# A graph network on one core: fewer column copies on ScalarE, and the placing of a chunk's sums ahead of the first layer

## The chip, the core and the metric

The kernel runs on one core of a Trainium2 chip. A core has TensorE (PE in the profile; its weight loads are PEld), VectorE (DVE), ScalarE (ACT), GpSimd (POOL) and SyncE (SP), which issues DMAs. Each engine takes its instructions in the order of its own program and waits on semaphores for the others. The metric is the device time of one execution in microseconds (us), lower is better.

## What is computed

One message-passing layer over a graph of 12,500 nodes with 128 features and 412,500 edges, sorted by their target node. The reference, cut to what matters (`x` has 32 scalars and 32 vectors of three a node):

```python
f0 = x0 @ W1_0e / np.sqrt(MUL)                      # and f1 from x1 with W1_1o
e0, e1 = feat0[edge_src], feat1[edge_src]           # rows gathered per edge
h = gelu(edge_scalar_attr @ W_mlp1 / np.sqrt(RADIAL))
h = gelu(h @ W_mlp2 / np.sqrt(HID))
w00, w01, w10, w11 = h @ Wp_00, h @ Wp_01, h @ Wp_10, h @ Wp_11
out0_a = w00 * e0 * ea0
out0_b = w11 * jnp.sum(e1 * ea1[:, None, :], -1) * INV_SQRT3
out1_a = (w01 * e0)[:, :, None] * ea1[:, None, :]
out1_b = w10[:, :, None] * e1 * ea0[:, :, None]
...
n0 = segment_sum(mid0, edge_dst) / np.sqrt(NUM_NEIGHBORS)   # and n1 from mid1
...
return layernorm(x + concat(y0, y1))
```

So each edge fetches the 128 features of its source node, multiplies them with weights that a small network makes of the edge's eight numbers, and adds the products to its target node.

## The kernel before

**Tiles.** The edges are cut into 806 runs of 512, a run into four quarters of 128 edges (one edge a partition). Two runs are a pair, four a chunk: 403 pairs and 202 chunks. The main loop `for p in range(NP)` handles one pair in each pass; `c` is the pair's chunk and `k` says whether the pair is the first (0, "even") or the second (1, "odd") of it. Four engines run an order that is written out by hand: what one pass calls, in the order in which it calls it, is each engine's program. POOL's gathers stand in the program's order too, ten pairs' buffers of G deep.

**Three ways to the source rows.** The features wanted by a quarter of a run normally come by one gather on POOL (`gather`, L223), which fetches 128 rows of a table in DRAM by their indices. A gather is issued nine pairs ahead, into the G buffer of the pair whose last message product has just been made, so the first gather of a pair waits for that product on VectorE. Every fourteenth run has one quarter fetched by SyncE with a DMA a row (`aid`, L208). And for some runs VectorE or ScalarE pick the columns themselves: all node features also lie transposed in SBUF (`xT`, a node a column), the address of a column is loaded into a register (`fetch`, L174), and a copy of one column of 128 numbers goes into a tile `gt` (`copy_columns`, L188 on VectorE, L192 on ScalarE). When a `gt` has its 128 columns, TensorE multiplies it with the weights and ScalarE copies the result into G (`picked_rows`, L197 and L198), and that quarter needs no gather.

**How many columns.** `SLOTS` says how many columns an engine copies in a pair, cut into slots between its other work, for even and odd pairs. `picked` is worked out from it at build time: from pair 6 on, an engine takes a further run as soon as its slots add up to 128 more columns. VectorE has 64 or 68 columns a pair and takes quarter 2 of a run now and then; ScalarE has 12, 16, 16 and 12 columns and takes quarter 1. `gather` leaves those quarters out.

**One pass for an even pair p = 2c,** with the lines as the profile names them:

- VectorE: `placing(c)` (L683) and `hot_rows(c + 1)` (L624); the first message product (L650); 24 columns; the second (L654); 20 columns; the third (L654); 20 columns. For an odd pair: the first two products; 24 columns; `select(c + 1)` (L639), which makes the segment weights of the next chunk; 16 columns; the third product; `add(c - 1)` (L710), which adds a placed chunk to the running sums; 28 columns.
- TensorE: `segments(p - 1)` (L670, 32 matmul records), `picked_rows` for runs two pairs ahead, `weights(p + 1)` (L597), `mlp1(c + 2)` (L554), then `place(c - 1)`, and now and then `moments` (L728, L731) of finished nodes. For an odd pair the second layer `mlp2(c + 2)` (L570) stands where `mlp1` stood, `radial` (L543) comes ahead of the weights, and there is no `place`.
- ScalarE: `segments_kept(p - 1)` (L676, copies the segment sums out of PSUM) with slot 0 of its columns; the copies into G (L198) and of the turned edge numbers (L545); slot 1; the first half of the layer's activation (`gelu1`, L559) with slot 2; `show(c + 1)` (L632, puts the edge attributes into PSUM for `select`); the second half of the activation with slot 3. For an odd pair the activation is `gelu2` (L576) and there is no `show`.

**`place(c)`** (L689 to L697) takes a chunk's four tiles of segment sums `SG` to their places among 96 nodes: it loads the four places into registers (L689), writes zeros with one matmul (L693), and adds four matmuls with the weights `SG` and the one-hot rows `PL` at places read from the registers (L697; eight matmul records). It writes into a PSUM tile called `bank` ("m" in the profile). The same tile holds the constant `numbers` (read by `placing` and `hot_rows`) and the area `shown` (written by `show`, read by `select`), and the order of use is kept for the tile as a whole: `select` waits for a `place` that stands ahead of it, and `place` for a `show` that stands ahead of it.

Of the kernel before, what the change touches and what calls it, by code (L numbers as in the profile page):

```python
# [15 lines left out]
ACT = mybir.EngineType.Activation  # L16
DVE = mybir.EngineType.DVE
# [28 lines left out]
AID_FROM = 36  # L46
AID_LEAD = 16
STEPS = 12
SLOTS = {DVE: ((24, 20, 20), (24, 16, 28)), ACT: ((12, 16, 16, 12), (12, 16, 16, 12))}
FROM = {DVE: 6, ACT: 6}  # L50
COL_Q = {DVE: Q - 2, ACT: Q - 3}
A_OF = (1, 2, 3, 0)
# [5 lines left out]
def gnn_kernel(ctx: ExitStack, tc: tile.TileContext, x, src, dst, ea4, ea8, w1_0, w1_1, wm1, wm2,  # L58
# [53 lines left out]

    per_chunk = {e: sum(map(sum, slots)) for e, slots in SLOTS.items()}
    picked = {}
    for e, slots in SLOTS.items():
        picked[e], done = [], 0
# [268 lines left out]
    for b in range(NG):  # L385
        c = math.ceil((min((b + 1) * GN, N) + MARGIN) / N * NCH) - 1
# [34 lines left out]
    def new_sums():  # L421
        A["next"] = wk.tile([P, 4, ACC], F32, name="acc")
# [519 lines left out]
    with tc.manual_schedule(engines={PE, ACT, DVE, SP}):  # L942
        load_raw_rows(nc.sync, 0, min(3, raw_runs))
        load_w1(nc.scalar)
        if raw_runs > 3:
            load_raw_rows(nc.scalar, 3, raw_runs)
        for s in range(min(LEAD - 2, raw_runs)):
            gather(s)
        nc.vector.tensor_scalar(ident, diag, 0.0, None, op0=OP.is_equal)
        nc.vector.tensor_copy(none[:, :P], iota)  # L950
        nc.vector.tensor_copy(bank[:, 4 * SPAN:4 * SPAN + P // 2], none[:, :P].bitcast(F32))
        for b in range(min(3, NG)):
            XT[b] = load_nodes(b)
        make_wf()
        clear()
        loads = list(weight_loads())
        new_sums()
        extra = {2: lambda: load_edges(0), 3: lambda: load_attributes(0), NG // 2 - 2: lambda: turn_attributes(0), 4: lambda: load_raws(0), NG // 2: lambda: load_indices(0),
                 NG // 2 + 3: make_w1b, NG // 2 + 5: make_ws, NG - 6: lambda: radial(0), NG - 4: lambda: networks(0),
                 NG - 2: lambda: networks2(0), NG - 1: make_wpost,  # L960
                 NG // 2 + 1: lambda: nc.vector.memset(A["next"], 0.0),
                 NG - 3: run_places}
        for b in range(NG + 2):
            if b < NG:
                turn(b)
            if 0 < b <= NG:
                features_of(b - 1)
            if 1 < b:
                store_nodes(nc.scalar, table, b - 2, PF[b - 2])
            if b + 3 < NG:  # L970
                XT[b + 3] = load_nodes(b + 3)
            if b > 4 and loads:
                nc.sync.dma_start(*loads.pop(0))
            if b in extra:
                extra[b]()
        assert not loads
        for c in range(1, min(EDGES_AHEAD, NCH)):
            load_edges(c)
        if aided:
            aid_load()  # L980
        for s in range(min(LEAD - 2, raw_runs), min(LEAD, NS)):
            gather(s)
        for c in range(1, min(3, NCH)):
            radial(c)
            if c == 1:
                networks(c)
                networks2(c)
        weights(0)
        show(0)
        hot_rows(0)  # L990
        select(0)
        for s in range(PR):
            turn_rows(s)
        for s in range(PR):
            features(s)
        A["now"] = A["next"]
        clearing = []
        placed = added = 0

        def picks(e, p, i, op=None):  # L1000
            if p < FROM[e]:
                if op:
                    op()
                return
            n = SLOTS[e][p % (CH // PR)][i]
            if not op:
                copy_columns(e, fetch(e, n))
                return
            first = fetch(e, n // 8 * 4)
            op()  # L1010
            copy_columns(e, first + fetch(e, n - n // 8 * 4))

        for p in range(NP):
            c, k = divmod(p, CH // PR)
            mine = [s for s in range(p * PR, (p + 1) * PR) if s < NS]
            if p:
                for s in mine:
                    if s + LEAD - PR < NS:
                        gather(s + LEAD - PR)
            if k == 1 and c + EDGES_AHEAD < NCH:  # L1020
                load_edges(c + EDGES_AHEAD)
            for s in mine:
                if s % P == P // 2 - 16 and (s // P + 1) * P < NS:
                    load_raws(s // P + 1)
                if s % P == P // 2 and (s // P + 1) * P < NS:
                    load_indices(s // P + 1)
                if s % ET == 8 and s - 8 + ET < NS:
                    load_attributes(s // ET + 1)
                for t in range(P // ROWS):
                    a = s + AID_LEAD - t * STEPS // (P // ROWS)  # L1030
                    if a in aided:
                        aid(a, t)
            nets = c + 2 < NCH
            if k == 0:
                placing(c)
                if c + 1 < NCH:
                    hot_rows(c + 1)
            if p:
                segments(p - 1)
                picks(ACT, p, 0, lambda: segments_kept(p - 1))  # L1040
            for e in picked:
                for s in mine:
                    if (e, s + 2 * PR) in pick_of:
                        picked_rows(e, pick_of[e, s + 2 * PR])
            if k == 1 and c + 3 < NCH:
                radial(c + 3)
            cleared = bool(late)
            rest = list(kept)
            norm_kept()
            picks(ACT, p, 1)  # L1050
            if p + 1 < NP:
                weights(p + 1)
            if nets:
                (mlp1, mlp2)[k](c + 2)
                picks(ACT, p, 2, lambda: (gelu1, gelu2)[k](c + 2, 0))
            else:
                picks(ACT, p, 2)
            if k == 0 and c + 1 < NCH:
                show(c + 1)
            for s in mine:  # L1060
                if s % ET == 20 and s - 20 + ET < NS:
                    turn_attributes(s // ET + 1)
            if nets:
                picks(ACT, p, 3, lambda: (gelu1, gelu2)[k](c + 2, 1))
            else:
                picks(ACT, p, 3)
            if k == 0 and c > 0:
                place(c - 1)
                placed = c
            raws_next = [s + PR for s in mine if s + PR < raw_runs]  # L1070
            for s in raws_next:
                turn_rows(s)
            messages(p, 0)
            if k == 0:
                picks(DVE, p, 0)
            messages(p, 1)
            picks(DVE, p, 1 - k)
            for s in raws_next:
                features(s)
            if rest:  # L1080
                norm_rest()
            if cleared:
                new_sums()
                clearing += list(range(4))
            elif clearing:
                clear_sums(clearing.pop(0))
            if k == 1 and c + 1 < NCH:
                select(c + 1)
            if k == 1:
                picks(DVE, p, 1)  # L1090
            messages(p, 2)
            if k == 1 and placed > added:
                add(added)
                added += 1
            picks(DVE, p, 2)
            if k == 0 and 0 < added == c - 1:
                norm(due.get(added - 1, []))
            if p == 0:
                addresses()
                find_first()  # L1100
                new_sums()
                clearing = list(range(4))
            if p == NP - 4:
                count_odd()
        finish_waiting()
        segments(NP - 1)
        segments_kept(NP - 1)
        if late:
            norm_kept()
            new_sums()  # L1110
            clearing += list(range(4))
        norm_rest()
        finish_waiting()
        for i in clearing:
            clear_sums(i)
        for c in range(added, NCH):
            if c >= placed:
                place(c)
            add(c)
            if c < NCH - 1 and c in due:  # L1120
                norm(due[c])
                norm_kept()
                norm_rest()
                finish_waiting()
        norm_last(due[NCH - 1])
# [31 lines left out]
```

## Time and profile before

| | us |
|---|---|
| runs of the kernel before | 5955.32, 5994.51, 5994.96 |
| median of them | 5994.51 |
| the profiled execution | 5962.68 |
| its span, first to last instruction | 5960.8 |
| mean granted clock of TensorE in it | 0.65 |

The profile's page gives busy time per engine, the chain of waits that ended last, and groups of instructions: line, engine, operation, tile written and tiles read, count, then total busy time and the mean of one in ns, then the idle time of the engine just ahead of them with what ended it. "Issue" there means that nothing in the profile explains the idle time; "remote" that a semaphore was raised by something that could not be told. A row of the timeline has the start and length in us, the engine and line, the count of merged instructions and, in brackets, the idle time before them and what ended it. POOL's gathers have rows of their own; the SyncE rows are left out of what is shown here, as are the weight loads of the timeline.

The profile's SyncE view holds 7040 single-row DMAs of `aid` (L208) beside the 2722 gathers by POOL from the table and 72 from the input.

### The profile page before, as it was taken

The numbers are of one execution on the slowest core, as the hardware profiler recorded it, in microseconds if no ns is written. First come the engines' busy times: TensorE is split into PE (matmuls) and PEld (weight loads), VectorE is DVE, ScalarE is ACT, GpSimd is POOL, SyncE is SP. The second block draws the span as 40 slices with busy tenths as digits, with TensorE's granted clock in tenths as the row PEclk, the third lists the DMA queues.
The fourth block names the chain that finished last, engine by engine and source line by source line (L and its number), as shares of the span: only waits on it lengthen the run. The fifth ranks groups of instructions, "written<-read, shape, count | busy, mean of one in ns | idle before, by whom it ended". The sixth has DMA issues, their size and how long they took to land. (4 is left out here: it accounts for less than half of the span.)

```text
span 5960.8 us, 141936 instructions
## 1 busy us (share of the span) xinstructions
PE 3407.7 (57%) x30231; PEld 2603.1 (44%) x30231; DVE 3366.2 (56%) x28706; ACT 3093.4 (52%) x24111; POOL 2636.3 (44%) x2801
## 2 busy tenths in 40 slices
PE   3665655556555555555556555556655555655556
PEld 2544444444444444444444444444434444443444
DVE  1265656555655555656555665566565555665556
ACT  0254555555555555555555555555554555555554
POOL 4344444444444444444444444444444444444441
PEclk5766666666666666666666666666666666666666
DMA  4211111111111111111111111111111111111111
GB/s 100 59 36 40 39 35 38 41 35 43 42 35 39 39 37 43 40 35 36 36 41 37 40 43 38 37 40 40 41 40 35 35 38 38 40 40 34 40 33 23
DMA packets 576979, 239.04 MB, mean 40 GB/s; under 512 B 481402, under 2 KB 526570, under 8 KB 576106
## 3 DMA queue, kind: packets, MB, share of 16 engines
q0 software_dynamic: 89408, 183.29, 10.8%
q1 hardware_dynamic: 465928, 40.14, 5.4%
q10 hardware_dynamic: 20770, 6.47, 0.5%
q14 instruction: 629, 5.15, 0.3%
q8 instruction: 244, 4.00, 0.3%
HBM read 216.86 MB, written 12.99 MB: 39 GB/s over the span
## 5 line engine op out<-in xcount | busy, mean ns | idle before, releaser
L223 POOL DMA_INDIRECT G<-table,idx x2722 | 2567.2, 943 | 3208.9 <-issue 1313.3
L192 ACT ACTIVATE gt<-xT 128x1 f32 x21888 | 2329.1, 189 | 924.5 <-issue 889.3
L188 DVE COPY gt<-xT 128x1 f32 x25984 | 1891.8, 145 | 1565.0 <-issue 1520.5
L670 PE MATMUL seg<-M,S 128*32 128x128 f32 x12896 | 845.7, 371 | 444.2 <-issue 426.8
L597 PE MATMUL w<-wpb,h 64*128 64x128 f32 x6448 | 855.1, 388 | 383.7 <-issue 383.1
L597 PEld LDWEIGHTS w<-wpb,h 64*128 64x128 f32 x6448 | 699.0, 277 | 554.6 <-issue 544.1
L670 PEld LDWEIGHTS seg<-M,S 128*32 128x32 f32 x12896 | 544.3, 148 | 692.1 <-issue 643.3
L654 DVE TENSOR_TENSOR M<-w,G 128x768 f32<-128x768 f32 x806 | 761.1, 945 | 2.7 <-issue 2.7
L676 ACT ACTIVATE sg<-seg 128x256 f32<-128x256 f32 x403 | 151.1, 375 | 1112.3 <-remote 777.6
L697 PEld LDWEIGHTS m<-pl,sg 128*128 128x128 f32 x1612 | 348.6, 312 | 797.7 <-issue 797.7
L693 PE MATMUL m<-none 128*128 128x384 bf16 x202 | 90.8, 450 | 786.1 <-ACT m L632 412.6
L554 PE MATMUL h<-eT,w1b 64*128 64x128 f32 x3232 | 439.3, 403 | 125.8 <-ACT G L198 95.9
L576 ACT ACTIVATE h<-h 128x512 f32<-128x512 f32 x404 | 237.1, 589 | 491.9 <-remote 377.0
L554 PEld LDWEIGHTS h<-eT,w1b 64*128 64x128 f32 x3232 | 394.3, 303 | 159.5 <-ACT G L198 120.5
L570 PE MATMUL h<-h,w2b 64*64 64x256 f32 x3232 | 393.5, 556 | 105.7 <-ACT G L198 68.7
L197 PE MATMUL h<-wf,gt 128*128 128x128 f32 x748 | 244.0, 411 | 268.2 <-issue 154.2
L650 DVE TENSOR_TENSOR M<-w,G 128x512 f32<-128x512 f32 x403 | 275.5, 684 | 204.1 <-remote 73.9
L697 PE MATMUL m<-pl,sg 128*128 128x128 f32 x1612 | 367.5, 404 | 0.0
L197 PEld LDWEIGHTS h<-wf,gt 128*128 128x128 f32 x748 | 162.8, 263 | 403.6 <-issue 246.9
L639 DVE TENSOR_TENSOR S<-oh,m 128x512 f32<-128x512 f32 x202 | 137.2, 679 | 356.7 <-PE m L697 251.4
L559 ACT ACTIVATE h<-h 128x512 f32<-128x512 f32 x404 | 234.6, 581 | 91.0 <-remote 37.9
L570 PEld LDWEIGHTS h<-h,w2b 64*64 64x64 f32 x3232 | 187.5, 186 | 214.9 <-ACT G L198 87.3
(123 smaller groups left out, 1592.5 us busy)
## 6 DMA issues: line engine op xcount, KB each, us to landing
G<-table SPq DMA_DIRECT2D x7040, 0.5 KB
G<-table,idx POOLq DMA_INDIRECT x2722
e<-in_edge_attr SPq DMA_DIRECT2D x201, 64.0 KB
xt<-in_x SPq DMA_DIRECT2D x24, 256.0 KB
table<-ft ACTq DMA_DIRECT2D x24, 256.0 KB
xt<-in_edge_attr SPq DMA_DIRECT2D x24, 256.0 KB
out<-y SPq DMA_DIRECT2D x24, 256.0 KB
xt<-in_dst SPq DMA_DIRECT2D x5, 256.0 KB
```

Of the source, the lines that this page charges most:

```text
L188: nc.vector.tensor_copy(to, col)
L192: nc.scalar.activation(to, col, AF.Copy)
L197: nc.tensor.matmul(pt, GT.pop((e, i)), wf, start=True, stop=True)
L223: nc.gpsimd.indirect_dma_start(out=G[s][:, q, :], out_offset=None, in_=x if s < raw_runs else table, in_offset=bass.IndirectOffsetOnAxis(a ...
L554: nc.tensor.matmul(p1[h][:, j // 2, j % 2, :], w1b[rows, j, :], eT[c][rows, :], start=True, stop=True)
L570: nc.tensor.matmul(p2[r][k * HID:(k + 1) * HID, h * n:(h + 1) * n], w2b[rows, :], H1[c][h][rows, k * n:(k + 1) * n], start=True, stop=True)
L576: nc.scalar.activation(H2[c][r].rearrange("p k j e -> p (k j e)"), P2[c][r], AF.Gelu_apprx_tanh, scale=1.0 / math.sqrt(HID))
L597: nc.tensor.matmul(WP[p][:, i, q, :], H2[c][q % 2][rows, k, q // 2, :], wpb[rows, :], start=True, stop=True)
L650: nc.vector.tensor_tensor(m[:, :, :, :MUL], w[:, :, :2 * MUL].rearrange("p q (a u) -> p q a u", a=2), g[:, :, None, :MUL].to_broadcast([P, ...
L654: nc.vector.tensor_tensor(m[:, :, j, MUL:].rearrange("p q (i u) -> p q i u", i=3), w[:, :, None, (2 + j) * MUL:(3 + j) * MUL].to_broadcast ...
L670: nc.tensor.matmul(SEG[c][q * W:(q + 1) * W, r + i, :], own[:, (r + i) * Q + q, h * W:(h + 1) * W], M[p][:, i, q, h, :], start=h == 0, sto ...
L697: nc.tensor.matmul(to[:, :, bass.ds(k_at, 4 * W)].bitcast(F32), SG[c][:, k, :], PL[c][:, k, :].rearrange("p (a n) -> p a n", a=4), start=F ...
```

## The change

Two edits. ScalarE's slots go from 12, 16, 16 and 12 columns a pair to four times 12, and since `picked` is worked out from them, fewer runs are picked on ScalarE and their quarters go back to POOL's gathers. And in an even pair `place(c - 1)` is called right behind `weights(p + 1)`, ahead of `mlp1(c + 2)`, instead of behind the calls of the activation and of `show(c + 1)`. The calls of the other engines keep their order.

```diff
-SLOTS = {DVE: ((24, 20, 20), (24, 16, 28)), ACT: ((12, 16, 16, 12), (12, 16, 16, 12))}
+SLOTS = {DVE: ((24, 20, 20), (24, 16, 28)), ACT: ((12, 12, 12, 12), (12, 12, 12, 12))}
...
             picks(ACT, p, 1)
             if p + 1 < NP:
                 weights(p + 1)
+            if k == 0 and c > 0:
+                place(c - 1)
+                placed = c
             if nets:
                 (mlp1, mlp2)[k](c + 2)
                 picks(ACT, p, 2, lambda: (gelu1, gelu2)[k](c + 2, 0))
...
             else:
                 picks(ACT, p, 3)
-            if k == 0 and c > 0:
-                place(c - 1)
-                placed = c
             raws_next = [s + PR for s in mine if s + PR < raw_runs]
```

## The prediction

> **What bounds the kernel now.** I read the page's head, the engine totals and the chain of waits first, then the costliest groups.
>
> ```profile
> span 5960.8 us, 141936 instructions
> PE 3407.7 (57%) x30231; PEld 2603.1 (44%) x30231; DVE 3366.2 (56%) x28706; ACT 3093.4 (52%) x24111; POOL 2636.3 (44%) x2801
> ACT 9%; another core or an unknown queue 5%; PE 5%; issue 4%; DVE 2%; ACTq 1%; DMA 1%; SPq 0%; DVEq 0%
> ...
> L223 POOL DMA_INDIRECT G<-table,idx x2722 | 2567.2, 943 | 3208.9 <-issue 1313.3
> L192 ACT ACTIVATE gt<-xT 128x1 f32 x21888 | 2329.1, 189 | 924.5 <-issue 889.3
> L188 DVE COPY gt<-xT 128x1 f32 x25984 | 1891.8, 145 | 1565.0 <-issue 1520.5
> ```
>
> No engine is full: the highest is 57%. The chain covers a quarter of the span only, so it can't name the limit. What stands out is idle time that nothing in the program explains ("issue") in front of the column copies on both VectorE and ScalarE. So I went on to the list of waits (total us, times, longest) and to the timeline of one stretch.
>
> ```profile
> DVE gt L188 <- issue: 1520.5, 2437, 1.7
> ACT sg L676 <- remote: 777.6, 128, 18.7
> PE m L693 <- ACT m L632: 412.6, 114, 10.9
> ACT sg L676 <- PE seg L670: 255.9, 86, 17.7
> DVE S L639 <- PE m L697: 251.4, 69, 9.3
> PE m L693 <- ACT h L559: 197.5, 42, 11.1
> DVE acc L710 <- ACT acc L428: 169.6, 15, 18.2
> DVE S L639 <- remote: 67.4, 14, 7.1
> ```
>
> VectorE waits for other engines in two places above all: `select` (L639) for 251.4 + 67.4 = 319 us, and `add` (L710) for 170 us. ScalarE waits 777.6 + 255.9 = 1033 us for the segment sums that it copies out at L676, so ScalarE has room and VectorE has little beyond these two and the "issue" time. TensorE waits 412.6 + 197.5 = 610 us ahead of `place` (L693), for ScalarE's `show` (L632) and the layer's activation (L559).
>
> ```profile
> 2269.72 0.85 PE L597 MATMUL w<-wpb,h 64*128 64x128 f32 x6
> ...
> 2271.01 0.21 DVE L188 COPY gt<-xT 128x1 f32 x2 [1.22 <-issue]
> ...
> 2276.70 0.46 DVE L188 COPY gt<-xT 128x1 f32 x6 [0.54 <-issue]
> 2276.88 0.38 ACT L676 ACTIVATE sg<-seg 128x256 f32<-128x256 f32 x1 [7.07 <-remote]
> 2277.07 0.95 DVE L654 TENSOR_TENSOR M<-w,G 128x768 f32<-128x768 f32 x1
> ...
> 2278.20 1.30 DVE L188 COPY gt<-xT 128x1 f32 x20 [0.18 <-issue]
> 2278.64 0.41 ACT L198 ACTIVATE G<-h 128x128 f32<-128x128 f32 x2
> 2278.78 0.94 POOL L223 DMA_INDIRECT G<-table,idx  x1 [3.75 <-ACT gt L192]
> 2278.95 2.23 PE L554 MATMUL h<-eT,w1b 64*128 64x128 f32 x16 [8.37 <-ACT G L198]
> 2279.25 1.59 ACT L192 ACTIVATE gt<-xT 128x1 f32 x16 [0.19 <-issue]
> ...
> 2280.02 0.95 POOL L223 DMA_INDIRECT G<-table,idx  x1 [0.30 <-issue]
> ...
> 2283.04 0.60 ACT L559 ACTIVATE h<-h 128x512 f32<-128x512 f32 x1 [2.20 <-remote]
> ...
> 2283.77 0.94 POOL L223 DMA_INDIRECT G<-table,idx  x1 [0.31 <-issue]
> ...
> 2286.27 0.94 POOL L223 DMA_INDIRECT G<-table,idx  x1 [0.30 <-issue]
> 2286.52 0.23 ACT L632 ACTIVATE m<-e 128x64 f32<-128x64 f32 x1 [0.51 <-issue]
> 2287.24 0.60 ACT L559 ACTIVATE h<-h 128x512 f32<-128x512 f32 x1 [0.49 <-issue]
> ...
> 2288.65 1.13 ACT L192 ACTIVATE gt<-xT 128x1 f32 x11 [0.50 <-issue]
> 2288.77 0.48 PE L693 MATMUL m<-none 128*128 128x384 bf16 x1 [7.59 <-ACT h L559]
> 2289.04 1.91 PE L697 MATMUL m<-pl,sg 128*128 128x128 f32 x8
> 2290.88 1.68 PE L670 MATMUL seg<-M,S 128*32 128x128 f32 x32
> 2291.06 0.69 DVE L639 TENSOR_TENSOR S<-oh,m 128x512 f32<-128x512 f32 x1 [7.90 <-PE m L697]
> 2292.27 1.06 DVE L188 COPY gt<-xT 128x1 f32 x16 [0.52 <-issue]
> ...
> 2293.25 0.95 DVE L654 TENSOR_TENSOR M<-w,G 128x768 f32<-128x768 f32 x1
> ```
>
> Two things are to be seen. First, **slow stretches**. A burst of gathers starts 0.76 us after the last message product of a pair (2277.07 + 0.95 = 2278.02, then 2278.78) and issues one gather every 1.25 us (0.94 + 0.30). From about its fifth gather to a little over a microsecond behind its last, the other engines get one or two instructions at a time: VectorE's eight columns from 2271.01 to 2276.70 took 0.71 us each, against 1.30/20 = 0.065 us at 2278.20; ScalarE's run at 1.59/16 = 0.099 us outside. That is the "issue" time. Each pair therefore costs its slow stretch plus whatever VectorE has not done outside it. Second, **a wait in series**: `show` at 2286.52, the layer's second activation, `place` from 2288.77 to 2290.95, and only then `select`, for which VectorE had been ready since 2283.15.
>
> **The change, part by part.** *Fewer columns on ScalarE.* In the code's own count, 48 columns a pair instead of 56 fill 147 runs instead of the 171 that the 21888 copies make (21888/128). 24 × 128 = 3072 copies go, with their register loads, 24 × 2 matmuls and 24 copies into G. At 0.099 us that is 304 us of ScalarE's time. I credit nothing of it, because ScalarE stands 1033 us at L676 waiting for TensorE; if that cover went, all 304 us would count.
>
> *24 more gathers on POOL.* Each is one more row at 1.25 us in a burst: 30 us. POOL itself has idle time before each burst (3.75 us in the stretch above), so the lower bound is 0; nothing speaks for less than that, as the gather takes no work off VectorE. It lengthens the slow stretch one for one, so I take 30. The Trainium skill, "DMA: Bandwidth & Descriptors", section "Anatomy of one DMA — SWDGE (gpsimd) path", puts a fixed cost of about 2.0 us on each such DMA; by that estimate the term would be 48 us, while the trace spaces them at 1.25.
>
> *`place` ahead of the first layer.* In the built order its first matmul then waits for VectorE alone (work at the start of the pair) and its third for ScalarE's copy L676, where it waited for `show` before. It brings a register load, the zeroing matmul, four address steps and eight matmul records.
>
> ```profile
> L689 PEldq TENSOR_LOAD <-rf x202: 328/337/521, 232.9 to 5937.8; - x101
> ```
>
> So 0.34 (the median) + (2289.04 + 1.91 − 2288.77 = 2.18) = 2.5 us of TensorE. The Trainium skill, "DMA: Bandwidth & Descriptors", section "Latency and other measured facts", gives a register load a floor of about 600 ns; this trace's 337 ns decides, and by the page `place` would be 0.26 us longer. Queued behind it on TensorE are `mlp1`, then the segment matmuls. In the stretch above the weights were done at 2270.57 and `mlp1` started at 2278.95, held by ScalarE's copy at L198; `place` could have started when L676 ended, at 2277.26, so 1.7 of its 2.5 us lie under that wait and `mlp1` is later by 0.8. Without the cover the first activation and all of ScalarE behind it come 2.5 us later; eight fewer columns ahead of `show` give 0.8 back.
>
> What goes: `select` waits for `show` alone. Here it could start at about 2286.8 instead of 2291.06. Its 0.69 us and two columns pass in the slow stretch, which ends at 2288.65; the other 14 columns take 0.9, and the product of 2293.25 starts at about 2289.6: 3.6 us, or 46% of the 7.9 us waited. 46% of 319 is 147 us. The bounds are 0 (`show` as late as `place` is now) and 319. I take 100, below the 147, since where `mlp1` has no cover `show` slips, and a slipped `show` has the slow stretch ahead of it.
>
> `add`'s 170 us wait for the copy of the sums (L428), which on ScalarE stands behind L676, and that behind the segment matmuls, which `place` no longer delays; only 15 of these waits exist. Between 0 and 170 I take 20, a little over 1 us each. The segment matmuls, ready for 2278.02 but run at 2290.88, also move ahead of the slow stretch; ScalarE's wait at L676 shrinks, which I credit with 0 as ScalarE is not the limit.
>
> The sum: +30 − 100 − 20 = −90 us. The profiled execution took 5962.7 us (span 5960.8), so 5872.7; the median of the runs lies 31.8 above it, hence **5905 us**.
>
> **Rivals.** *The wait only changes hands* (28%). `mlp1` is 2.5 us later in most chunks, twelve columns stand between the activation and `show`, and `show` ends where `place` ends now. For it: `show` is already inside the slow stretch above. Against it: even there `show` ended 4 us before `place`. Left is the cost of the gathers: 5994.5 + 30 = 6025. That `place` moved and still starts late for another reason is counted here; the built order shows none.
>
> *Slower: `show` falls into the slow stretch* (19%). It decides where `show` comes behind the fifth gather of its burst. Then the twelve columns before it cost 0.71 instead of 0.099 us each, 7.3 us. If that happens in a third of the 202 chunks, 67 × 7.3 = 489 us of new waiting at L639 replace 319; the 170 more, at 46%, are 78, with the gathers 108: 6102. For it: TensorE's 2.5 us stand between the end of one slow stretch and the start of the next. Against it: the eight columns fewer, and segment matmuls and weights that also move forward, so that `place` itself starts earlier in the following pairs.
>
> *ScalarE is the limit after all* (6%): 5994.5 + 30 − 304 = 5720. The chain of waits names it most; its 1033 us at L676 speak against.
>
> **How the numbers follow.** The forecast has 47%. A measurement of this kernel can tell about 1%, or 60 us, from no change. With its terms between their bounds the forecast runs from 5830 (147 for `select`, 50 for `add`) to 5990 (+30 with next to nothing gained), three quarters of it under 5935. Faster by over 1%: 0.35 + 0.06 = 0.41. Within 1%: 0.12 from the forecast and 0.25 from the first rival, 0.37. Slower: 0.19 + 0.03 = 0.22. The range 5830 to 6060 takes in the forecast and the first rival and leaves out the ScalarE case and the upper part of the slower one. The forecast's own range is 5830 to 5990.
>
> **What would show it.** POOL's L223 group grows by 24 and the 1.25 us spacing stays. The wait of L639 for L697 is gone from the list of waits; what is left of it is put down to L632 or "remote" and is under half of 319 us. L693's 610 us of waits for L632 and L559 go; what is left names L676 or VectorE. The segment matmuls start within 3 us of the last message product in the even pairs. L676's wait shrinks by some hundreds of us. The forecast is wrong if `show` starts later against the burst than now, if L639 still waits 300 us, or if "issue" before L188 grows by more than the 30 us of gathers.

## The result and the profile after

| | kernel before | changed kernel |
|---|---|---|
| runs | 4: 5955.32 to 5994.96 us | 4: 5809.59 to 5823.09 us |
| median | 5985.1 us | 5813.95 us |
| ratio to before, 95% interval | 1 | 0.9724 [0.9685, 0.9764] |
| profiled execution, its span | 5962.68, 5960.8 us | 5816.3, 5814.5 us |

The changed kernel is faster by 2.8% by this ratio; the two medians alone give 0.971. The direction was forecast. The size was not: 5813.95 lies 16 us under the low end of the range, 5830.

The head of its page, the engine totals and the gathers:

```profile
span 5814.5 us, 138736 instructions
PE 3382.2 (58%) x30183; PEld 2473.8 (43%) x30183; DVE 3374.6 (58%) x28705; ACT 2769.8 (48%) x21015; POOL 2660.0 (46%) x2825
...
L223 POOL DMA_INDIRECT G<-table,idx x2746 | 2591.0, 944 | 3043.0 <-issue 1287.3
```

ScalarE has 323.6 us less to do (3093.4 before), POOL has its 24 gathers more. VectorE is as busy as it was, so the time came out of its idle time. Its groups before (the columns, L188, stand in the prediction):

```profile
L650 DVE TENSOR_TENSOR M<-w,G 128x512 f32<-128x512 f32 x403 | 275.5, 684 | 204.1 <-remote 73.9 <-ACT G L615 70.5 <-issue 42.6
L639 DVE TENSOR_TENSOR S<-oh,m 128x512 f32<-128x512 f32 x202 | 137.2, 679 | 356.7 <-PE m L697 251.4 <-remote 67.4 <-issue 36.8
L710 DVE TENSOR_TENSOR acc<-m,acc 128x384 f32 x202 | 110.9, 549 | 208.9 <-ACT acc L428 169.6 <-ACT y L741 23.8 <-issue 14.1
```

and after:

```profile
L188 DVE COPY gt<-xT 128x1 f32 x25984 | 1904.1, 145 | 1640.9 <-issue 1601.0 <-DMA G<-table,idx 7.1 <-remote 1.7
L650 DVE TENSOR_TENSOR M<-w,G 128x512 f32<-128x512 f32 x403 | 275.6, 684 | 173.3 <-ACT G L615 85.8 <-remote 54.7 <-issue 26.6
L639 DVE TENSOR_TENSOR S<-oh,m 128x512 f32<-128x512 f32 x202 | 136.8, 677 | 167.6 <-ACT m L632 99.4 <-issue 51.9 <-ACT h L559 7.1
L710 DVE TENSOR_TENSOR acc<-m,acc 128x384 f32 x202 | 110.9, 549 | 189.3 <-ACT acc L428 137.1 <-ACT y L741 34.8 <-issue 16.3
```

The number behind the bar is busy time, the last block is idle time and what ended it. Of VectorE's time, L639 from 356.7 to 167.6 is −189.1, L650 −30.8, L710 −19.6; the columns at L188 give back 1640.9 − 1565.0 = +75.9; busy time is +8.4 (3374.6 − 3366.2), and all the small groups together are +9. That is the 146.3 us by which the span shrank. Such an account adds up for any engine, so it says where VectorE's time went and not that this wait set the time. `select` no longer names `place` (L697) at all, but mostly `show` (L632).

ScalarE's groups say what became of its 324 us, before (the columns, L192, stand in the prediction):

```profile
L676 ACT ACTIVATE sg<-seg 128x256 f32<-128x256 f32 x403 | 151.1, 375 | 1112.3 <-remote 777.6
L576 ACT ACTIVATE h<-h 128x512 f32<-128x512 f32 x404 | 237.1, 589 | 491.9 <-remote 377.0
L559 ACT ACTIVATE h<-h 128x512 f32<-128x512 f32 x404 | 234.6, 581 | 91.0 <-remote 37.9
```

and after:

```profile
L192 ACT ACTIVATE gt<-xT 128x1 f32 x18816 | 1979.0, 189 | 492.1 <-issue 458.1
L676 ACT ACTIVATE sg<-seg 128x256 f32<-128x256 f32 x403 | 152.4, 378 | 1116.7 <-remote 858.3
L576 ACT ACTIVATE h<-h 128x512 f32<-128x512 f32 x404 | 237.4, 589 | 645.4 <-remote 488.0
L559 ACT ACTIVATE h<-h 128x512 f32<-128x512 f32 x404 | 237.4, 588 | 492.4 <-remote 234.0
```

The idle time ahead of the layer's activation grew, from 91 to 492 us at L559 and from 492 to 645 at L576; ahead of the columns (L192) it fell from 924.5 to 492.1, and ahead of L676 it stayed (1112, now 1117). With 323.6 us less to do in a span shorter by 146.3, ScalarE stands idle 177 us longer. A stretch of the timeline with the new order:

```profile
3004.06 0.38 ACT L676 ACTIVATE sg<-seg 128x256 f32<-128x256 f32 x1 [0.29 <-remote]
3004.10 2.08 PE L597 MATMUL w<-wpb,h 64*128 64x128 f32 x16
...
3006.12 0.50 PE L693 MATMUL m<-none 128*128 128x384 bf16 x1
3006.41 1.92 PE L697 MATMUL m<-pl,sg 128*128 128x128 f32 x8
3006.42 0.95 DVE L654 TENSOR_TENSOR M<-w,G 128x768 f32<-128x768 f32 x1
...
3008.13 0.94 POOL L223 DMA_INDIRECT G<-table,idx  x1 [6.25 <-ACT gt L192]
...
3009.76 1.58 PE L670 MATMUL seg<-M,S 128*32 128x128 f32 x30
...
3012.83 0.20 ACT L632 ACTIVATE m<-e 128x64 f32<-128x64 f32 x1
...
3013.80 0.69 DVE L639 TENSOR_TENSOR S<-oh,m 128x512 f32<-128x512 f32 x1 [1.28 <-ACT m L632]
```

`place` runs right behind the weights, beside VectorE's product, and is over at 3008.33, ahead of the burst's slow part. The segment matmuls follow the pair's last product by 2.39 us (3009.76 − 3007.37); worked out for 185 even pairs of each trace, the median went from 6.5 to 1.6 us, and the share under 3 us from 6% to 79%. `select` starts 0.77 us behind the end of `show`.

### The profile page after: what moved, and what is told of

The parts are those of the page before. It is cut to its first block, busy times and chain, and to the rows that moved or that the text cites. A ratio compares the mean times of both kernels' runs of the same rounds, so it can differ in the third digit from the quotient of the medians.

```text
span 5814.5 us, 138736 instructions
## 1 busy us (share of the span) xinstructions
PE 3382.2 (58%) x30183; PEld 2473.8 (43%) x30183; DVE 3374.6 (58%) x28705; ACT 2769.8 (48%) x21015; POOL 2660.0 (46%) x2825
## 5 line engine op out<-in xcount | busy, mean ns | idle before, releaser
L188 DVE COPY gt<-xT 128x1 f32 x25984 | 1904.1, 145 | 1640.9 <-issue 1601.0
L192 ACT ACTIVATE gt<-xT 128x1 f32 x18816 | 1979.0, 189 | 492.1 <-issue 458.1
L597 PEld LDWEIGHTS w<-wpb,h 64*128 64x128 f32 x6448 | 719.9, 290 | 502.1 <-issue 491.4
L670 PEld LDWEIGHTS seg<-M,S 128*32 128x32 f32 x12896 | 499.1, 132 | 987.2 <-issue 806.5
L676 ACT ACTIVATE sg<-seg 128x256 f32<-128x256 f32 x403 | 152.4, 378 | 1116.7 <-remote 858.3
L570 PE MATMUL h<-h,w2b 64*64 64x256 f32 x3232 | 456.9, 617 | 333.8 <-ACT eT L545 143.2
L576 ACT ACTIVATE h<-h 128x512 f32<-128x512 f32 x404 | 237.4, 589 | 645.4 <-remote 488.0
L559 ACT ACTIVATE h<-h 128x512 f32<-128x512 f32 x404 | 237.4, 588 | 492.4 <-remote 234.0
L570 PEld LDWEIGHTS h<-h,w2b 64*64 64x64 f32 x3232 | 211.7, 206 | 477.6 <-ACT eT L545 184.8
L697 PEld LDWEIGHTS m<-pl,sg 128*128 128x128 f32 x1612 | 331.7, 286 | 117.2 <-issue 70.3
L650 DVE TENSOR_TENSOR M<-w,G 128x512 f32<-128x512 f32 x403 | 275.6, 684 | 173.3 <-ACT G L615 85.8
L697 PE MATMUL m<-pl,sg 128*128 128x128 f32 x1612 | 341.8, 375 | 57.5 <-ACT sg L676 37.9
L554 PE MATMUL h<-eT,w1b 64*128 64x128 f32 x3232 | 305.6, 333 | 28.4 <-ACT G L198 12.0
L554 PEld LDWEIGHTS h<-eT,w1b 64*128 64x128 f32 x3232 | 260.3, 233 | 68.1 <-issue 30.8
L639 DVE TENSOR_TENSOR S<-oh,m 128x512 f32<-128x512 f32 x202 | 136.8, 677 | 167.6 <-ACT m L632 99.4
L710 DVE TENSOR_TENSOR acc<-m,acc 128x384 f32 x202 | 110.9, 549 | 189.3 <-ACT acc L428 137.1
```

The source lines that it names most:

```text
L188: nc.vector.tensor_copy(to, col)
L192: nc.scalar.activation(to, col, AF.Copy)
L554: nc.tensor.matmul(p1[h][:, j // 2, j % 2, :], w1b[rows, j, :], eT[c][rows, :], start=True, stop=True)
L559: nc.scalar.activation(H1[c][h], P1[c][h].rearrange("p k j e -> p (k j e)"), AF.Gelu_apprx_tanh, scale=1.0 / math.sqrt(RAD))
L570: nc.tensor.matmul(p2[r][k * HID:(k + 1) * HID, h * n:(h + 1) * n], w2b[rows, :], H1[c][h][rows, k * n:(k + 1) * n], start=True, stop=True)
L597: nc.tensor.matmul(WP[p][:, i, q, :], H2[c][q % 2][rows, k, q // 2, :], wpb[rows, :], start=True, stop=True)
```

## The experiments

The kernel before takes very different times on different chips: about 5985 us on the chip of the result, 6049.5 on the one of the g runs, and 3876 to 3885 on the four of all other runs below. So each ratio stands against the kernel before on the same chip, and two groups of chips have to be read apart. That the chip itself makes the difference, and not something else that changed between the measurements, isn't shown.

The expectations name theories by letters. **A**: VectorE's wait for `place` at L639 is what goes, ScalarE has room, and a gather costs 1.25 us. **B**: ScalarE's columns are the cost. **C**: the two edits need each other. Two were formed on the way. **D**: a loop through ScalarE and TensorE (segment copy, columns, activation, `show`, `place`, segment matmuls, segment copy) sets the time, and either edit opens it; behind it stands POOL. **E**: the slow stretches decide, by whether `show` stands behind the burst's fifth gather.

### First four: each edit alone, and each cost by itself

`place` moved and ScalarE left at 56 columns:

```diff
+            if k == 0 and c > 0:
+                place(c - 1)
+                placed = c
             if nets:
                 (mlp1, mlp2)[k](c + 2)
...
-            if k == 0 and c > 0:
-                place(c - 1)
-                placed = c
```

> The placing moved, ScalarE's slots left at 12, 16, 16, 12 (171 runs, 2722 gathers from the table). Theory A (VectorE's wait for the placing is what went; ScalarE has room; a gather costs its 1.25 us): the whole gain and 24 gathers fewer, 5814 - 30 = about 5785, ratio to the kernel before about 0.967, and L639 idle under 180 us. Theory B (ScalarE's 304 us of columns are what went, the move only matters little): about 5950, ratio 0.995. Theory C (the two need each other: with 56 columns the attributes' copy L632 comes too late behind the moved placing): about 5900, with L639 waiting 250 us or more, now for L632.

48 columns on ScalarE, `place` where it was:

```diff
-... ACT: ((12, 16, 16, 12), (12, 16, 16, 12))}
+... ACT: ((12, 12, 12, 12), (12, 12, 12, 12))}
```

> ScalarE's slots at four times 12 (147 runs, 2746 gathers from the table), the placing left behind the network's first layer. Theory A: only the 24 gathers are left, 5985 + 30 = about 6015, ratio 1.005, L639 idle about 350 us as before. Theory B: about 5850, ratio 0.98. Theory C: a small gain, about 5930, ratio 0.99.

The changed kernel, with a second copy of every third column of slots 1 and 2 into a tile that nothing reads (3136 copies):

```diff
...
+                if again and at % 3 == 0:
+                    more.append(at)
+                    k = len(more) % 64
+                    nc.scalar.activation(spare[:, k:k + 1], col, AF.Copy)
...
```

> The changed kernel with 8 further column copies a pair on ScalarE (4 each in slots 1 and 2) into a spare tile, with no register loads of their own and with no gather saved: some 3100 more copies, 0.099 us each, 307 us of ScalarE's time. Theory A: ScalarE has room, within 20 us of the changed kernel, 5815 to 5835. Theory B: most of the 307 us come back, 5950 or more. Theory C: L632 is later by 0.8 us and more where it falls into a slow stretch, 5850 to 5900, with L639's idle time up by 60 us or more.

The kernel before, with 49 gathers more into a tile that nothing reads:

```diff
+            if q == 0 and s % 16 == 1 and s >= 32:
+                nc.gpsimd.indirect_dma_start(
+                    out=spare_rows, out_offset=None, in_=table,
+                    in_offset=bass.IndirectOffsetOnAxis(ap=rows, axis=0))
```

> The kernel before with 49 more gathers, one in every sixteenth run, into a spare tile that nothing reads. It measures what one gather costs. The price in the forecast, 1.25 us each: +61 us, 5985 + 61 = 6046, ratio 1.010. Covered by POOL's idle time: 0, ratio 1.000. At 2.0 us each: +98 us, ratio 1.016.

| beside the kernel before at 3877.3 us | median us | ratio, 95% |
|---|---|---|
| `place` moved alone | 3587.0 | 0.925 [0.9218, 0.9282] |
| 48 columns alone | 3607.5 | 0.9312 [0.9278, 0.9345] |
| both, and 3136 copies | 3573.5 | 0.9227 [0.9195, 0.9259] |
| before, and 49 gathers | 3878.7 | 0.9995 [0.9972, 1.0018] |

Each edit alone brings some 7%, so C fell on these chips, and so did A, by which 48 columns alone bring nothing. The copies put back cost nothing next to both edits (0.9208, below), so B, by which the columns are a cost by themselves, fell in this plain form; but that was seen only where both edits had been made and, as shown below, something else sets the time. The 49 gathers cost nothing, so on these chips POOL had idle time in the kernel before. The last run can stand for the kernel before, which has the same time. Its page and its waits (its lines are numbered one higher up to L224 and five higher behind, so L224 is the gathers, L681 the copy of the sums, L698 and L702 `place`, L644 `select`):

```profile
PE 2606.4 (67%) x30231; PEld 2075.7 (54%) x30231; DVE 3161.4 (82%) x28706; ACT 2889.0 (75%) x24111; POOL 2685.2 (69%) x2850
L681 ACT ACTIVATE sg<-seg 128x256 f32<-128x256 f32 x403 | 151.6, 376 | 618.6 <-PE seg L675 602.4
```

```profile
ACT sg L681 <- PE seg L675: 602.4, 209, 8.2
PE m L698 <- ACT m L637: 524.1, 194, 8.7
DVE S L644 <- PE m L702: 108.2, 103, 2.6
```

ScalarE waits for the segment matmuls, which stand on TensorE behind `place`, which waits for `show`, which ScalarE does. Its busy 2889.0, its 618.6 at L681 and its 168.7 ahead of the columns make 3676 of the span of 3873. VectorE's wait at `select` is only 108 us, while the time that either edit saves is 270 to 290. This is theory D: moving `place` takes it out of the loop, eight columns fewer make the loop shorter. The 3072 copies fewer are 304 us by the prediction's 0.099 us each; 270 were gained.

### Is it POOL behind the loop, and what else opens it

The changed kernel itself:

> The changed kernel itself, beside the single edits. Where the kernel before takes about 3877 us, as in the first four runs: theory D (a loop through ScalarE and TensorE: segment copy, columns, activation, L632, placing, segment matmuls; either edit opens it, and behind it stand POOL's gathers at 1.248 us each without a gap): 2818 gathers are 3517 us and about 55 us around them, 3572, ratio 0.921, no faster than either edit alone by more than 40 us. If the edits added, 0.925 x 0.931 = 0.861, 3340 us. Where it takes about 5985 us: 0.972 as before, and the slow stretches are back in the timeline.

`place` moved ahead of `show` only, behind the layer on TensorE, ScalarE at 56 columns:

```diff
+            if k == 0 and c > 0:
+                place(c - 1)
+                placed = c
             if k == 0 and c + 1 < NCH:
                 show(c + 1)
...
-            if k == 0 and c > 0:
-                place(c - 1)
-                placed = c
```

> The kernel before (56 columns) with the call of the placing moved up by a few lines only, to stand ahead of show: on TensorE it stays behind the first layer, but no longer waits for L632. Theory D: the wait was all, as fast as the placing ahead of the layer, ratio 0.925 (3587 where before takes 3877). If the place ahead of the layer is what counts, half the gain at most, ratio 0.96 or more. Theory A (VectorE's wait at L639): the same as theory D, and L639 idle under 180 us.

The changed kernel with the 49 gathers of above:

> The changed kernel with 49 more gathers into a spare tile. Theory D: POOL has no idle time left, so each costs its 1.248 us, 61 us more than the changed kernel beside it (3633 where that takes 3572). If VectorE, busy 88% there, is the limit: the same time as the changed kernel, within 15 us. Where the kernel before takes about 5985 us, 61 us more as well if the gathers' slow stretches set the time.

`place` moved, and ScalarE at 64 columns:

```diff
+... ACT: ((16, 16, 16, 16), (16, 16, 16, 16))}
```

> The placing moved and ScalarE's slots raised to four times 16 (196 runs, 49 gathers fewer than the changed kernel). Theory D: POOL is relieved by 61 us and the loop is open, so faster than both: about 3515 where the changed kernel takes 3572, ratio 0.907. If ScalarE's 64 columns close the loop again: 3600 or more, ratio 0.93 or more.

| beside the kernel before at 3878.8 us | median us | ratio, 95% |
|---|---|---|
| the changed kernel | 3568.4 | 0.9208 [0.9172, 0.9245] |
| `place` ahead of `show`, 56 columns | 3555.7 | 0.917 [0.9129, 0.9211] |
| the changed kernel, and 49 gathers | 3691.7 | 0.9522 [0.9483, 0.956] |
| `place` moved, 64 columns | 4036.8 | 1.0406 [1.0363, 1.0449] |

`place` moved up by a few lines only, still behind the layer but ahead of `show`, brings as much as the whole change. So on these chips its wait for `show` was what counted, not its place ahead of the layer. The changed kernel's page here:

```profile
PE 2509.7 (70%) x30183; PEld 1907.2 (54%) x30183; DVE 3150.8 (88%) x28705; ACT 2641.1 (74%) x21015; POOL 2666.0 (75%) x2825
...
L223 POOL DMA_INDIRECT G<-table,idx x2746 | 2596.3, 945 | 845.7 <-issue 743.6
...
L188 DVE COPY gt<-xT 128x1 f32 x25984 | 1702.1, 144 | 213.3 <-issue 185.9
```

A gather takes 0.945 us and 0.3 us stand ahead of it: (2596.3 + 845.7) / 2746 = 1.253 us each, start to start. From 300 us on, all steps between gathers that are longer than 1.3 us exceed 1.248 by 1.6 us together; in the kernel before with spare gathers that sum was 218.2 us, of which up to 77.3 are the spare gathers' waits for each other. POOL issues without a gap, and its 75% is a full engine. The page's busiest engine is VectorE at 88%. The Trainium skill, "Perfetto Trace Analysis", section "Identifying the Most-Contended Engine", would take that one for the limit; here the gapless gathers decide against it.

The spare gathers confirm that. Where POOL had gaps they cost nothing, here 123 us:

```profile
L224 POOL DMA_INDIRECT G<-table,idx x2746 | 2592.7, 944 | 844.3 <-issue 741.4 <-DMA G<-table,idx 56.4 <-DMA flat<-in_src 7.2
...
L228 POOL DMA_INDIRECT spare<-table,idx x49 | 46.2, 943 | 85.0 <-DMA spare<-table,idx 75.4 <-issue 5.6 <-DMA G<-table 2.0
```

The spare gathers' own row holds 46.2 + 85.0 = 131 us. 75.4 of them are the wait of each for the landing of the last one in the same tile, which the kernel's own gathers with ten buffers hardly have. So the run overstates a gather's price: theory D had said 61 us, 49 × 1.25, and the other half of the 123 us is this wait.

With 64 columns the kernel is slower than before. Theory D's forecast of 0.907 for the open loop missed; what holds is the other case on record, that 64 columns close a loop again:

```profile
PE h L197 <- ACT gt L192: 436.3, 186, 4.2
ACT h L559 <- PE h L554: 420.1, 184, 5.4
DVE S L639 <- ACT m L632: 289.9, 143, 3.3
```

Here the layer comes late, the columns stand ahead of `show`, and `select` waits 290 us for `show`. It is the prediction's slower rival without a slow stretch: moving `place` works as long as ScalarE is not filled up in its place.

### More row DMAs on SyncE in place of gathers

SyncE fetches a quarter in every ninth run instead of every fourteenth, which takes 31 gathers off POOL, in the kernel with `place` ahead of `show`, the same with 48 columns, and the kernel before:

```diff
-AID = 14
+AID = 9
...
-STEPS = 12
+STEPS = 9
```

> 56 columns, the placing ahead of show but behind the layer, and SyncE fetching one quarter in every ninth run instead of every fourteenth: 86 runs instead of 55, so 31 gathers fewer (2763 in all) and 3968 more single-row DMAs on SyncE. Theory D (POOL without a gap is the limit behind the loop): 31 x 1.248 = 39 us less than with every fourteenth, 3556 - 39 = 3517 where the kernel before takes 3878, ratio 0.907. If VectorE, busy 88 to 89%, is the limit: no change, ratio 0.917. If SyncE cannot keep up: above 3556.

> The same with ScalarE's slots at four times 12 (2787 gathers). Theory D: 24 gathers more than its neighbour with 56 columns, +30 us, 3547, ratio 0.915. If ScalarE's columns still count behind the opened loop: faster than its neighbour.

> The kernel before with only SyncE's share raised to every ninth run, 31 gathers fewer. Theory D: the loop through ScalarE is the limit there and POOL waits for it, so no change where the kernel before takes 3878, ratio 1.00, within 10 us. If gathers cost their 1.25 us in the kernel before: 39 us less, ratio 0.990. Where the kernel before takes about 5985 us and the gathers' slow stretches set the time: 39 us less or more, ratio 0.993.

Against 3875.6 us they took 4979.5 (1.2841 [1.2812, 1.2871]), 4965.5 (1.2815 [1.2787, 1.2844]) and 4976.6 us (1.2835 [1.2806, 1.2864]). All three are alike, so the runs tell nothing of the change, nor of theory D's forecasts for 31 gathers fewer (0.907, 0.915 and 1.00); what came is the case that SyncE can't keep up. The waits of the third:

```profile
PE h L543 <- DMA e<-in_edge_attr: 1019.9, 169, 15.1
ACT eT L545 <- PE h L543: 831.7, 178, 13.9
DVE M L650 <- PE w L597: 596.4, 121, 12.9
```

The edge numbers, which SyncE loads as well, stand behind its row DMAs in its program: at 2499.91 us 26 of these took 9.70 us, and only then an edge load was issued. TensorE waited for the edge numbers 169 times, 1020 us in all, and the others for TensorE. It made another bound.

### Three runs with slow stretches

These ran on a chip like that of the result: ScalarE at 52 and at 60 columns with `place` where it was, and `place` ahead of `show` with 48 columns:

```diff
+... ACT: ((12, 14, 14, 12), (12, 14, 14, 12))}
...
+... ACT: ((12, 18, 18, 12), (12, 18, 18, 12))}
```

> The kernel before with ScalarE's slots at 12, 14, 14 and 12 (159 runs, 12 gathers more), the placing where it was. Theory D (the loop through ScalarE is the limit and each column in it costs its 0.099 us in every pair): 4 columns x 0.099 x 397 pairs = 157 us less, ratio 0.959 (3720 where before takes 3877). If four fewer columns only move the work to a better place: anything else than half of the 0.931 of eight. Where the kernel before takes about 5985 us: theory A +15 us, ratio 1.002; theory D again 157 us less, ratio 0.974.

> The same in the other direction: 12, 18, 18 and 12 (184 runs, 13 gathers fewer). Theory D: 157 us more, ratio 1.041. If POOL or VectorE is the limit: the same or up to 16 us less, ratio 0.996. Where the kernel before takes about 5985 us: theory A 16 us less, ratio 0.997; theory D ratio 1.026.

> Both edits, but with the placing ahead of show and behind the layer on TensorE. Theory D: POOL's gathers are the limit, 24 more of them than with 56 columns: 3556 + 30 = 3586, ratio 0.925 (the changed kernel gave 0.921 there). Where the kernel before takes about 5985 us: the wait for L632 is gone and the layer is not delayed by the placing, so as fast as the changed kernel or faster, ratio 0.972 or less; if the order ahead of the layer is what counts there, 0.985 or more.

| beside the kernel before at 6049.5 us | median us | ratio, 95% | idle ahead of L639, us |
|---|---|---|---|
| 52 columns | 6171.2 | 1.0185 [1.0142, 1.0227] | 583.3 |
| 60 columns | 6737.0 | 1.1158 [1.1104, 1.1212] | 1247.2 |
| `place` ahead of `show`, 48 columns | 5821.7 | 0.962 [0.9589, 0.965] | 72.2 |
| (on the result's chip) before | | 1 | 356.7 |
| (on the result's chip) changed | | 0.9724 | 167.6 |

`select` in the 60-column kernel:

```profile
L639 DVE TENSOR_TENSOR S<-oh,m 128x512 f32<-128x512 f32 x202 | 138.6, 686 | 1247.2 <-PE m L697 1228.7 <-issue 18.3
```

and in the third:

```profile
L639 DVE TENSOR_TENSOR S<-oh,m 128x512 f32<-128x512 f32 x202 | 136.5, 676 | 72.2 <-issue 64.7 <-ACT m L632 4.8 <-ACT eT L545 0.8
```

Where there are slow stretches, the time and this one wait stand in the same order over all five kernels. Taking 356.7 us for the kernel before here too (its trace is of the other chip), the 60-column kernel loses 687.5 us for 890.5 of waiting, 0.77 us a us; the third gains 227.8 for 284.5, 0.80; the 52-column kernel loses 121.7 for 226.6, 0.54. The order alone doesn't make the wait the cause. The "issue" time ahead of ScalarE's own columns (L192) stands in it too: 418.4, 458.1, 889.3, 1597.5 and 1684.9 us, from the fastest kernel to the slowest. A ScalarE that is held up brings `show` later, and with it `place` and `select`; these runs don't tell which of the two waits sets the time. `place` ahead of `show` came out within its forecast, 0.972 or less.

That 52 columns are slower than 56 was not expected, and no theory gave it. For 60 columns theory A had 0.997 and D 1.026, so neither gave the size of that loss. The program loads a slot of 14 as 4 addresses ahead of the activation and 10 behind it, a slot of 16 as 8 and 8, a slot of 18 as 8 and 10; whether the larger load behind the activation is the cause was not tried.

Theory E can be held against these traces. `show` started behind the fifth gather of its burst in 55 of 185 chunks of the kernel before, in 57 of the 52-column kernel and in 164 of the 60-column one. These chunks hold 215 of the 350, 323 of the 561 and 1118 of the 1188 us that `select` waited in the 185. So a later `show` fits the loss with 60 columns, but not the one with 52, where it was as often late as before.

### The single edits again

`place` moved alone and 48 columns alone, and later `place` ahead of `show` with 56 columns and 48 columns alone, repeated in the hope of a chip with slow stretches:

> The placing moved and 56 columns kept, a second time, for a chip where the kernel before takes about 6000 us (the first time it took 3877). There, theory A (the wait at L639 sets the time, 0.77 us for each us of it): the wait falls at least as far as in the changed kernel and 24 gathers fewer, ratio 0.96 to 0.97. Theory E (the slow stretch decides: with 56 columns the placing ahead of the layer pushes L632 behind the fifth gather): L639 idle 300 us or more, ratio 0.99 to 1.03. Where the kernel before takes 3877: 0.925 again.

> Four times 12 columns and the placing left in place, a second time, for such a chip. Theory A: the placing still waits for L632, which comes some 0.8 us earlier; L639 idle 250 to 350 us, ratio 0.98 to 1.005. Theory E: eight columns fewer ahead of L632 keep it out of the slow stretch, L639 idle under 200 us, ratio 0.97 to 0.98, nearly the whole gain of the change. Where the kernel before takes 3877: 0.931 again.

> 56 columns with the placing ahead of show, behind the layer, a second time. Where the kernel before takes about 6000 us: theory A, the wait at L639 is gone without any fewer columns, idle under 150 us, ratio 0.95 to 0.965, as with 48 columns (0.962) or 0.005 better for its 24 gathers fewer; theory E, 56 columns keep L632 in the slow stretch, idle 250 us or more, ratio 0.98 to 1.01. Where it takes 3877: 0.917 again.

> Four times 12 columns alone, a third time, for a chip where the kernel before takes about 6000 us: theory A: L639 idle 250 to 350 us, ratio 0.98 to 1.005. Theory E: L639 idle under 200 us, ratio 0.97 to 0.98. Where it takes 3877: 0.931 again.

Both times it was a chip without them, the same one. Against 3885.1 us: `place` moved 3589.6 (0.9231 [0.9213, 0.925]), 48 columns 3616.2 (0.9316 [0.9291, 0.9341]). Against 3883.2: `place` ahead of `show` 3562.3 (0.9163 [0.9129, 0.9197]), 48 columns 3621.1 (0.9325 [0.929, 0.936]). They repeat the earlier ratios on another chip to 0.002 and leave open how the 0.9724 divides between the edits where the slow stretches are. `place` ahead of `show` with the columns left alone is no slower than the changed kernel on the chip where both ran; their intervals overlap there (0.917 and 0.9208), so it is not shown to beat it.

## Why the prediction missed the size

**The step that failed is the size of the term for `select`: 147 us were worked out, and 100 taken.** The mechanism fits the trace: `place` no longer stands between `show` and `select`, and VectorE's wait for it is gone. That this wait, and not the fewer columns, made the 2.8% isn't shown, since neither edit ran alone where the slow stretches are.

From one pair the prediction worked out that 46% of the 319 us would come off, 147. In that pair the wait itself would shrink by 4.3 of its 7.9 us, and 3.6 us, the 46%, were left once the columns that VectorE then reaches earlier had passed in the slow stretch. It took 100 only, because a later `show` would have the slow stretch ahead of it, and let the range end at 147 though the term's own bound was 319. Measured, the idle time of L639 fell by 189.1 us and that of the columns at L188 grew by 75.9. With 30 of the 75.9 for the gathers, as forecast, 46 are left for such columns, and the term was worth 189 − 46 = 143 us, 45% of 319. How the 75.9 divide wasn't measured; with all or none of them for such columns the term is 113 or 189, both above 100. So the discount had no ground: `show` did come later, and it cost little (below). That one pair out of 403 came so close to the share is luck as far as these runs tell.

L650 gave 31 us that were not forecast. In the same sum, +30 − 143 − 20 − 31 and +17 for busy time and small groups make −147, against 146 measured and 90 forecast.

**A second term failed beside it: the 31.8 us** by which the median of the kernel before lay above its profiled execution, added to the sum without a reason why the changed kernel should show it. The changed kernel's profiled execution, 5816.3, lies 2.4 us above its median. So of the 91 us between the forecast and the measurement, some 56 are in the sum and some 34 in this addition. With 146 in the sum and the 31.8 kept, the time would have been 5848, inside the range; without the 31.8 the range would have begun near 5798 and held the measured time.

**The gathers.** 24 more and the 1.25 us spacing are as forecast. "Issue" ahead of L188 grew by 80.5 us (1601.0 − 1520.5), more than the 30 that the prediction set as a sign of failure. The sign was badly chosen, since this time also holds the columns that VectorE reaches earlier. In the five kernels with slow stretches it runs against the wait at L639, and not with the gathers: 1772.1, 1601.0, 1520.5, 1411.3 and 1285.7 us, from the shortest wait to the longest, with 2746, 2746, 2722, 2734 and 2709 gathers.

**`show` against the burst.** The prediction called itself wrong if `show` came later in the burst, and the slower rival hung on that in a third of the chunks. It did come later. In 185 chunks of each trace, `show` started 2.4 us (median) behind the start of the last burst before the change and 4.6 us after it, and behind that burst's fifth gather in 55 chunks before and 71 after. But in those 71 `select` waited 1.4 us on average, where it had waited 3.9 in the 55, now that it no longer waits for a `place` behind `show`. So the rival's condition held and its price, 7.3 us a chunk, did not. Its mechanism is real all the same: with 64 columns and `place` moved (4% slower, for `show`) and with 60 and `place` where it was (12% slower, for `place` behind `show`), `select` waits longer.

**The first rival**, that the wait only changes hands, fell: 99.4 us of the waiting at L639 now name `show`, against 318.8 us that went.

**ScalarE, credited with nothing.** On the result's chip the sum comes out without it, but 48 columns alone never ran on such a chip, so it isn't shown. The forecast that L676's wait shrinks by hundreds of us was wrong; it stood at 1117, although TensorE's waits ahead of `place` went. So there this wait had another reason, which stays open. On the chips without slow stretches the same 24 runs taken off ScalarE are worth 7% by themselves, since there ScalarE's work lies on the loop that sets the time. There the cover named in the prediction, waiting for TensorE, was a part of that loop and no free time: the wait at L676 was for matmuls that waited, by way of `place`, for ScalarE itself.

**`add`** gave its 20 us (208.9 to 189.3). The segment matmuls moved ahead as the prediction said, and the 610 us of TensorE's waits at L693 for `show` and the activation are gone.

## What to carry to other kernels

An engine that waits a long time isn't free if what it waits for waits for it: follow the wait round before crediting its work with nothing, and look for the cheapest place to open the loop, which on the chips without slow stretches was either of the two edits. Where a tile is ordered as a whole, put the producer that nobody needs soon ahead of the one that somebody is waiting for. Don't take a discount off a term for a danger that no trace has priced, and let the range reach that term's bounds. And a difference between one profiled execution and the median of a few runs need not carry over to another kernel: it belongs in the range and not in the sum.

## What the runs showed of the hardware

The same program ran 1.5 times as long where the result and the g runs were measured as on the four other chips, 5985 and 6049 us against 3876 to 3885. The work is the same: the column copies take 145 and 144 ns each. What differs is the time between them, 1601 us of "issue" ahead of L188 in the changed kernel on the one chip and 185.9 us on the other. TensorE's mean granted clock was 0.68 in the first and 0.83 in the second, but VectorE's and ScalarE's columns are held up as well. Worked out from the traces of both, a gather's last packet starts 2.2 and 2.1 us behind the gather, so the transfers themselves are hardly slower. Between the fifth gather of a burst and the end of its last, TensorE, VectorE and ScalarE together start 6 instructions a us in the first trace, weight loads counted; in the second they start 32 a us, with the gathers running all the time. Why instructions come so slowly during a burst of gathers in the one case stays open.

A gather's start-to-start price of 1.25 us is what POOL can issue, well under the time to landing: the spare gathers into one tile waited 75 us for each other on top. The Trainium skill, "DMA: Bandwidth & Descriptors", section "Anatomy of one DMA — SWDGE (gpsimd) path", puts the fixed 2.0 us of such a DMA mostly on its completion, not on its setup; by this, gathers into different buffers may follow each other faster than that, and the 1.25 us agrees.
